# Moving the low-rank product, the evacuations and the late weight combinations of an adaptive FFN kernel

## The chip, the cores and the metric

One Trainium2 chip, one of its cores. The time is device microseconds of the whole program, the median of several runs. One execution of it was taken by the hardware profiler; times of single instructions come from that one, in microseconds from its start.

## The reference, cut to what matters

```python
# cond: a quantised weight with a low-rank part
lora_delta = lora_B @ lora_A * (32.0 / 64)               # rank 64, 2048 x 2048
cb    = codebook / max(abs(codebook))                    # 32 levels
scale = exp(scale_log)                                   # one per row and group of 128
normalized = (weight + lora_delta).reshape(O, I // 128, 128) / scale
thresholds = (cb[:-1] + cb[1:]) * 0.5
quantized  = cb[searchsorted(thresholds, normalized)]
w = (quantized - normalized) + normalized                # "straight through"
c = x @ ((w * scale).reshape(O, I) + lora_delta).T
# ffn: a dense layer, and 8 experts of rank 16 mixed by a router
result = c @ W_base.T + b_base
probs  = softmax(c @ router_w.T)
mixed  = einsum(einsum(c @ A_w.T, cores), probs)
out = x + result + (mixed @ B_w.T) * 2.0
```

x has 4096 rows of 2048, everything is float32.

## The kernel before, in words

The two dense layers and the residual are merged into one 2048 x 2048 matrix, M = W_base (w_q + delta) + identity, so that x meets only one large product. The program has three stretches.

**First stretch, the matrix (to about 1172 us).** It is built in 16 *strips* of 128 columns (loop at L755). Each strip quantises its 128 x 2048 piece of weight: for each of 27 thresholds ACT writes a mask (`raise_to`, L549: a Relu with a huge gain) and DVE writes the next level where the mask is set (L550, `copy_predicated`). The masks lie in a ring of four. The four lowest levels are not done by these passes, but ahead of time: ACT does level 0, and level 3 of half 0, in three parts each (`scalar_level`: Relu L516, Sign L519, then L521 or L524), GpSimd does levels 1 and 2, and sometimes 3, and adds them (`pool_levels` L534 and L535, `last_level` L539). From strip 6 on level 3 of half 1 is a half-width pass of DVE instead. While strip i goes through its passes, the other engines do:

- for strip i + 1: PE the low-rank product in two halves (`delta`, L410; both use the same PSUM tile), ACT its scaling (`scaled`, L502), GpSimd adding it and dividing by the scale (`normalize`, L504 to L507), and then the levels above;
- for strip i - 1: GpSimd turns the levels back into a weight (`straight_through`, L572 to L574, in two halves; in the last strip DVE in four quarters), PE multiplies it with W_base in two pairs of output blocks, (2, 0) and then (3, 1), in four quarters each (`products`, L621, `low_rank`, L609), PE the router's rows (`multiply_router`, L634 and L639; `router_sum`, L650), ACT copies the blocks out of PSUM and a DMA stores them (`keep`, L654 and L655);
- for strip i - 2: the last quarter of its (3, 1), and PE's router product with x (`route`, L674);
- from strip 5 on: GpSimd makes the sums of the finished columns that the fast product of the third stretch needs (`outer_w` L320, `inner_w` L329 to L332), and SP stores them (`put`, L351 to L353).

**Order of the work.** The program is in a manual schedule: each engine does its instructions in the order in which they are written. `behind(step, f, ...)` puts a piece of work after pass `step` of the strip; that fixes only its place in the queue of each engine that it uses. SP issues most DMAs in that order; GpSimd and ACT issue some of their own.

**Passage (1172 to about 1290 us).** After the last strip PE does its (2, 0), then its (3, 1). GpSimd fetches, sums and puts the sums of the first product's last quarter (`first_fetch` and so on). `late_columns` (L714) takes blocks 0 and 2 of the last group of strips: it fetches them into a buffer of 128 x 8192 ("late"), DVE makes the outer and inner sums of each block, and GpSimd issues the 32 DMAs that put them to DRAM. Then come the blocks 1 and 3 (`last_fetch`, L310 on SP for 1 and on GpSimd for 3, `last_outer`, `last_inner`, `last_put`), which the loop of the third stretch runs beside. The buffer of block 3 lies in memory that "late" used.

**Third stretch, the product (to the end).** x M is computed for four groups of 1024 tokens by a fast method of two levels, 7 x 7 = 49 products in each group (`product`, L954), with DVE, ACT and GpSimd adding up the results (`after`, L1034 to L1045) from four PSUM buffers. DVE's queue has, after the first terms of x, the sums of blocks 1 and 3 ("last"), then a difference of x (L917, xB), and then L1036 (u2), which frees the PSUM buffer that the seventh product needs.

The functions that the change touches, and where they are called:

Of the kernel before, what the change touches and what calls it, by code (L numbers as in the profile page):

```python
# [10 lines left out]
F32 = mybir.dt.float32  # L11
# [10 lines left out]
P = 128  # L22
# [6 lines left out]
NL = 4  # L29
# [154 lines left out]
def adaln_ffn_kernel(  # L184
# [29 lines left out]
    nc = tc.nc  # L214
    D, N = xT.shape
    NS, _, NM, _ = weight.shape
# [31 lines left out]
    NK = NS // 4  # L248
    HB = NK * 2

    strip = [j * NK + k for k in range(NK) for j in range(4)]
# [103 lines left out]
    def last_outer(b):  # L355
        outer_w(nc.vector, NK - 1, b)

    def last_inner(b, ms, z):
        inner_some(nc.vector, NK - 1, b, ms, z)

    def last_put(b, *sets):
        for ms in sets:
            put(NK - 1, b, ms, nc.gpsimd)


    with ExitStack() as sa:
# [22 lines left out]
        strips = {}  # L389
# [172 lines left out]
            assert not at, at  # L562

        def straight_through(i):
            last = i == NS - 1
            n = 4 if last else 2
            for h in range(n):
                m = ts(h, NM // n)
                w, a = strips[i]["w"][:, m, :], strips[i]["a"][:, m, :]
                sc = scale[:, strip[i], m].unsqueeze(2).to_broadcast([P, NM // n, P])  # L570
                v = nc.vector if last else nc.gpsimd
                v.tensor_tensor(a, a, w, ALU.subtract)  # L572
                v.tensor_tensor(a, a, w, ALU.add)  # L573
                v.tensor_tensor(a, a, sc, ALU.mult)  # L574
# [73 lines left out]
        def router_sum(i):  # L648

            nc.tensor.matmul(strips[i]["r"][:, P : P + RP], raw, stack, start=True, stop=True)  # L650

        def keep(i, b):
            out = spool.tile([P, 4, BC], F32, tag="out", name=f"out_{i}_{b}")
            nc.scalar.copy(out.rearrange("p q c -> p (q c)"), strips[i][b])  # L654
            (nc.scalar if i == NS - 1 else nc.sync).dma_start(wc_dram[i // 4][b][:, i % 4], out)  # L655

        def keep_router(i):
            nc.scalar.copy(rac[:, strip[i], :], strips[i]["r"][:, P : P + RP])
# [55 lines left out]
        def late_columns():  # L714

            t = big0.tile([P, NM, OQ], F32, tag="wb", name="late").rearrange("p m o -> p (m o)")
            for n, b in enumerate((0, 2)):
                f = t[:, 3584 * n : 3584 * n + 3584]
                columns(NK - 1, b, f[:, 0:2048], f[:, 2048:3584])
                fetch(NK - 1, b, range(3))  # L720
            for b in (0, 2):
                fetch(NK - 1, b, (3,))
            for b in (0, 2):
                if b == 0:
                    z = ypool.tile([P, 2048], F32, tag="up", name="late_z0")
                    z = (z[:, 0:1024], z[:, 1024:2048], t[:, 7168:8192])
                else:
                    more = ypool.tile([P, 1536], F32, tag="more", name="late_z1")
                    z = ypool.tile([P, 2048], F32, tag="up", name="late_z2")
                    z = (more[:, 0:1024], z[:, 0:1024], z[:, 1024:2048])  # L730
                last_outer(b)
                last_inner(b, (5, 6), z[0])
                last_inner(b, (2, 7), z[1])
                last_inner(b, (3,), z[2][:, 0:512])
                last_inner(b, (4,), z[2][:, 512:1024])
                last_put(b, (5, 6), (2, 7), (3,), (4,))


        made = {5: [(0, 0)], 6: [(0, 1)], 7: [(0, 2)], 8: [(0, 3)], 9: [(1, 0)], 10: [(1, 1)],
# [15 lines left out]
        for i in range(NS):  # L755
            at = {}

            def behind(r, f, *args):
                at.setdefault(r, []).append(lambda: f(*args))

            if i > 1:

                products(i - 2, (3, 1), NC - 1)
                route(i - 2, 0)
                behind(0, load_route, i - 2, 1)
                behind(2, keep, i - 2, 3)
                behind(3, keep, i - 2, 1)
            if i + 1 < NS:
                delta(i + 1, 0)
                if i > 0:  # L770
                    behind(1, load_w, i + 1, 2)
                behind(4, scaled, i + 1, 0)
                behind(4, normalize, i + 1, 0)
                behind(10, scaled, i + 1, 1)
                behind(10, normalize, i + 1, 1)
                for r, f, parts in ((0, 0, (11, 12, 13)), (NL - 1, 0, (14, 15, 18)), (0, 1, (19, 20, 21))):
                    for n, p in enumerate(parts):
                        behind(p, scalar_level, i + 1, f, r, n)
                behind(14, pool_levels, i + 1, 0)
                behind(19, last_level, i + 1, 0)  # L780
                behind(21, pool_levels, i + 1, 1)
            if i > 0:


                behind(9, load_route, i - 1, 0)
                if i == NS - 1:
                    behind(9, load_route, i - 1, 1)
                for c in range(2):
                    behind(2 + 3 * c, products, i - 1, (2, 0), c)
                if i + 1 < NS:  # L790
                    behind(7, delta, i + 1, 1)
                if i > 1:
                    behind(8, route, i - 2, 1)
                for c in range(2, NC):
                    behind(2 + 3 * c, products, i - 1, (2, 0), c)
                behind(13, multiply_router, i - 1)
                behind(16, keep, i - 1, 2)
                behind(17, keep, i - 1, 0)
                for c in range(NC - 1):
                    behind((17, 20, 22)[c], products, i - 1, (3, 1), c)  # L800
                behind(19, router_sum, i - 1)
                behind(23, keep_router, i - 1)
                behind(18, router_parts, i - 1)
                if i + 2 < NS:
                    behind(20, load_la, i + 2)
            else:
                behind(3, nc.vector.reciprocal, rflat[:, NM:], flat[:, NM:])
                behind(7, delta, i + 1, 1)
                behind(22, lora_columns, 0)
                behind(24, lora_columns, 1)  # L810
                behind(25, lora_router)
            for n, (g, b) in enumerate(made.get(i, [])):
                step_of = (3, 5, 10, 13, 17, 23, 25) if len(made[i]) == 1 else (
                    (4, 6, 8, 9, 10, 12, 13) if n == 0 else (17, 19, 21, 22, 23, 24, 25)
                )
# [12 lines left out]

                behind((0, 14)[n], begin, g, b)
                r = step_of  # L830
                behind(r[0], outer_w, nc.gpsimd, g, b)
                behind(r[1], inner_pair, g, b, PAIRS[0])
                behind(r[1], inner_pair, g, b, PAIRS[1])
                behind(r[2], put, g, b, PAIRS[0])
                behind(r[3], put, g, b, PAIRS[1])
                behind(r[4], inner_pair, g, b, PAIRS[2])
                behind(r[4], inner_pair, g, b, PAIRS[3])
                behind(r[5], put, g, b, PAIRS[2])
                behind(r[6], put, g, b, PAIRS[3])
            quantize(i, at)  # L840
            straight_through(i)

# [24 lines left out]
        for h in range(2):  # L867
            route(last, h)
# [412 lines left out]
```

## Time and profile before

| | |
|---|---|
| median of 3 runs | 2670.41 us (2669.06 to 2674.28) |
| the profiled execution | 2666.77 us, its span 2665.0 us |
| granted TensorE clock, mean | 0.975 of full speed |
| PE busy | 2503.9 us, 94% of the span |
| DVE busy | 1549.0 us, 58% |
| GpSimd busy | 1367.2 us, 51% |
| ACT busy | 1130.1 us, 42% |
| L550 on DVE, 448 passes | 1090.2 us busy |
| L549 on ACT, 448 masks | 872.4 us busy |
| DMA | 581 MB, 218 GB/s mean |

The page cuts the span into 40 slices of about 66.6 us. Each digit is the busy share in tenths:

```profile
PE   5499999999999999999999999999999999999999
DVE  9999999999999999973433223242133332224221
ACT  7899999999999999930000000000000000000000
POOL 5777778889888888745313140042320323202224
PEclk9799999999999999999999999999999999999999
```

PEclk is the clock that PE was granted, in tenths. The shares are averages over a slice: PE's 9 in the first stretch has some 5 us of idle time in each strip. In a row of the timeline, the numbers are start and duration, then engine, line, operation, shapes and how many instructions are taken together; in brackets stands the idle time of the engine before it and what ended it. In a row of the chain of waits there are start, duration and what was at work.

### The profile page before, as it was taken

How to read it: one execution, taken by the hardware profiler on the slowest of the kernel's cores; microseconds unless marked ns; L12 is line 12 of the kernel's file. 1: busy time of each engine (PE TensorE's matmuls, PEld its weight loads, DVE VectorE, ACT ScalarE, POOL GpSimd, SP SyncE). 2: the span in 40 equal slices, each digit the busy share in tenths (PEclk: the TensorE clock that was granted, in tenths of full speed). 3: DMA queues.
4: the chain of work that ended last, by engine and by line, in shares of the span. 5: the costliest groups of instructions: out<-in, count | busy, mean ns of one | idle time of the engine just before them, and what ended most of it. 6: DMA issues, size and time to landing. Idle time of an engine off the chain costs nothing.

```text
span 2665.0 us, 26423 instructions
## 1 busy us (share of the span) xinstructions
PE 2503.9 (94%) x10576; PEld 1704.1 (64%) x10576; DVE 1549.0 (58%) x990; ACT 1130.1 (42%) x796; POOL 1367.2 (51%) x783
## 2 busy tenths in 40 slices
PE   5499999999999999999999999999999999999999
PEld 2244444444444444345888888888888888888887
DVE  9999999999999999973433223242133332224221
ACT  7899999999999999930000000000000000000000
POOL 5777778889888888745313140042320323202224
PEclk9799999999999999999999999999999999999999
DMA  8255457776777777699844666536675455854554
GB/s 317 102 177 185 168 181 252 233 241 228 234 243 249 235 231 227 217 327 347 323 174 173 218 245 232 187 142 213 244 234 194 157 206 177 279 208 173 194 199 158
DMA packets 225979, 581.08 MB, mean 218 GB/s; under 512 B 20600, under 2 KB 121728, under 8 KB 182720
## 3 DMA queue, kind: packets, MB, share of 16 engines
q1 hardware_dynamic: 219296, 557.96, 61.1%
q0 software_dynamic: 4960, 14.95, 1.6%
q10 hardware_dynamic: 1600, 6.49, 0.7%
q8 instruction: 83, 1.36, 0.2%
q14 instruction: 40, 0.33, 0.0%
HBM read 477.62 MB, written 101.71 MB: 217 GB/s over the span
## 4 chain that ended last, share of the span: by engine, by line
PE 62%; ACT 17%; DVE 8%; POOL 7%; DMA 3%; issue 2%; SPq 0%; DVEq 0%; ACTq 0%; POOLq 0%
PE z L954 49%; ACT above L549 11%; PE m L621 10%; DVE a L550 7%; ACT sg L516 2%; ACT sg L519 2%; POOL a L572 1%; POOL a L573 1%; PE z L984 1%; ACT a L521 1%; POOL lv L534 1%; POOL a L574 1%; POOL a L535 1%; DMA xA<-in_xT 1%; DMA wc_dram<-out 1%
## 5 line engine op out<-in xcount | busy, mean ns | idle before, releaser
L550 DVE COPY_PREDICATED a<-above,step 128x2048 f32<-128x2048 uint8 (+1 forms) x448 | 1090.2, 2436 | 61.1 <-ACT above L549 19.3
L549 ACT ACTIVATE above<-w,neg_t 128x2048 fp8e5<-128x2048 f32 (+1 forms) x448 | 872.4, 1976 | 55.1 <-DVE a L550 44.5
L954 PE MATMUL z<-t,s 128*128 128x256 f32 x3584 | 791.4, 380 | 2.0 <-DVE u L1036 1.7
L954 PEld LDWEIGHTS z<-t,s 128*128 128x128 f32 x3584 | 677.5, 190 | 105.5 <-issue 13.2
L621 PE MATMUL m<-wbp,a 128*128 128x512 f32 x1024 | 502.1, 636 | 115.0 <-POOL a L574 101.0
L621 PE MATMUL m<-wb,a 128*128 128x512 f32 x1024 | 462.1, 594 | 4.4 <-ACT out L654 4.4
L621 PEld LDWEIGHTS m<-wbp,a 128*128 128x128 f32 x1024 | 202.6, 204 | 370.9 <-issue 239.7
L621 PEld LDWEIGHTS m<-wb,a 128*128 128x128 f32 x1024 | 194.5, 191 | 247.1 <-issue 242.4
L1034 ACT COPY m<-z 128x1024 f32<-128x1024 f32 x28 | 28.4, 1013 | 759.2 <-PE z L954 759.2
L1045 POOL TENSOR_TENSOR c<-u,m 128x1024 f32<-128x1024 f32 x16 | 50.1, 3130 | 443.8 <-DVE u L1042 422.4
L954 PE MATMUL z<-xA,s 128*128 128x256 f32 x1152 | 254.6, 379 | 0.0
L534 POOL TENSOR_SCALAR lv<-w,past,rise 128x1024 f32<-128x1024 f32 x65 | 245.9, 3783 | 3.7
L954 PEld LDWEIGHTS z<-xA,s 128*128 128x128 f32 x1152 | 218.8, 190 | 30.5 <-issue 0.8
L1045 POOL TENSOR_TENSOR M<-u,m 128x1024 f32<-128x1024 f32 x8 | 24.5, 3068 | 328.9 <-DVE u L1042 288.2
L954 PE MATMUL z<-xC,s 128*128 128x256 f32 x768 | 169.7, 379 | 0.0
L954 PE MATMUL z<-xB,s 128*128 128x256 f32 x768 | 169.7, 379 | 0.0
L535 POOL TENSOR_TENSOR a<-a,lv 128x1024 f32<-128x1024 f32 x65 | 154.3, 2374 | 27.1 <-ACT a L521 21.0
L1036 DVE TENSOR_TENSOR u<-z,m 128x1024 f32<-128x1024 f32 x28 | 34.3, 1224 | 218.5 <-issue 175.0
L1040 ACT COPY m<-z 128x1024 f32<-128x1024 f32 x28 | 28.3, 1011 | 308.8 <-PE z L954 308.8
L954 PEld LDWEIGHTS z<-xC,s 128*128 128x128 f32 x768 | 145.9, 190 | 19.8
L954 PEld LDWEIGHTS z<-xB,s 128*128 128x128 f32 x768 | 145.9, 190 | 19.8
L1042 DVE TENSOR_TENSOR u<-z,u 128x1024 f32<-128x1024 f32 x28 | 34.3, 1223 | 119.8 <-PE z L954 81.3
(213 smaller groups left out, 1958.0 us busy)
## 6 DMA issues: line engine op xcount, KB each, us to landing
s<-s_dram SPq DMA_DIRECT2D x196, 1024.0 KB, 4.9
wbp<-in_wbT SPq DMA_DIRECT2D x131, 1024.0 KB, 5.4
xs<-in_xT SPq DMA_DIRECT2D x64, 512.0 KB, 6.5
xA<-in_xT SPq DMA_DIRECT2D x24, 1024.0 KB, 9.4
s_dram<-z SPq DMA_DIRECT2D x84, 256.0 KB, 6.2
xB<-in_xT SPq DMA_DIRECT2D x16, 1024.0 KB, 10.4
outT<-M SPq DMA_DIRECT2D x16, 1024.0 KB, 12.5
w<-in_weight SPq DMA_DIRECT2D x30, 512.0 KB, 5.2
```

The lines of the kernel that those rows point to most:

```text
L516: nc.scalar.activation(strips[i]["sg"], q, AF.Relu, bias=neg_t[:, r : r + 1], scale=GAIN)
L519: nc.scalar.activation(sg, sg, AF.Sign)
L534: v.tensor_scalar(lv, half(i, f, "w"), past[:, r : r + 1], rise[:, r : r + 1], ALU.is_gt, ALU.mult)
L535: v.tensor_tensor(a, a, lv, ALU.add)
L549: nc.scalar.activation(above[:, c], q, AF.Relu, bias=neg_t[:, r : r + 1], scale=GAIN, saturate=False)
L550: nc.vector.copy_predicated(a, above[:, c].bitcast(U8), step[:, r : r + 1].to_broadcast([P, F // n]))
L621: nc.tensor.matmul(ps, strips[i]["a"][:, CM * c + m, :], t[:, m, :], start=c == 0 and m == 0, stop=False)
L954: nc.tensor.matmul(z[:, c, :], s[:, k, ts(c, P)], rhs[:, k, :], start=not more and k == 0 and c % PER == 0, stop=k == NK - 1 and c % PER = ...
L1034: nc.scalar.copy(temp("m1", o), z["a"])
L1036: nc.vector.tensor_tensor(temp("u2", o), z["b"], state["m1", o], ALU.add)
L1042: nc.vector.tensor_tensor(temp("u3", o), z["d"], state["u2", o], ALU.add)
L1045: lambda d: nc.gpsimd.tensor_tensor(d, state["u3", o], state["m5", o], ALU.add),
```

## The change

It moves work and splits some; the passes, the products and the sums stay the same.

- `straight_through` on GpSimd works in a quarter, a quarter and a half of the strip's width, instead of two halves.
- The second half of the low-rank product (`delta(i + 1, 1)`) comes behind the first quarter of (2, 0) instead of the second; the quarters of (2, 0) are put behind steps 4, 6, 8, 11 (before 2, 5, 8, 11), `scaled` at 3 and 7 (4 and 10), `normalize` at 5 and 9 (4 and 10).
- The passes of the lowest levels come in another order and at other steps; `pool_levels` at 13 and 19 (14 and 21), `last_level` at 23 (19).
- `keep` of blocks 2 and 0 at 14 and 15 (16 and 17), of block 1 at 4 (3); `router_sum` at 20 and `keep_router` at 24 (19 and 23).
- The combinations' steps: outer sums at 4 (3), inner pairs at 8, 10, 24, 25 (5, 5, 17, 17), puts at 10, 12, 25, 26 (10, 13, 23, 25).
- In the passage both blocks are copied out of PSUM first, then the router's part, then both stores are issued on ACT's queue; the router's sum comes after the first quarter of (3, 1).
- `late_columns`: both blocks' outer sums first; block 0's inner sums on DVE, block 2's sixteen inner operations on GpSimd, in two batches; the eight puts of the second batch come last.

```diff
-    def last_inner(b, ms, z):
-        inner_some(nc.vector, NK - 1, b, ms, z)
+    def last_inner(b, ms, z, v=nc.vector):
+        inner_some(v, NK - 1, b, ms, z)
...
         def straight_through(i):
             last = i == NS - 1
-            n = 4 if last else 2
-            for h in range(n):
-                m = ts(h, NM // n)
+            v = nc.vector if last else nc.gpsimd
+            for m in (0, 4), (4, 8), *(((8, 12), (12, 16)) if last else ((8, 16),)):
...
-        def keep(i, b):
+        def evacuate(i, b):
             out = spool.tile([P, 4, BC], F32, tag="out", name=f"out_{i}_{b}")
             nc.scalar.copy(out.rearrange("p q c -> p (q c)"), strips[i][b])
-            (nc.scalar if i == NS - 1 else nc.sync).dma_start(wc_dram[i // 4][b][:, i % 4], out)
+            strips[i]["out", b] = out
+
+        def store(i, b, q=nc.sync):
+            q.dma_start(wc_dram[i // 4][b][:, i % 4], strips[i]["out", b])
+
+        def keep(i, b):
+            evacuate(i, b)
+            store(i, b)
...
                 last_outer(b)
-                last_inner(b, (5, 6), z[0])
-                last_inner(b, (2, 7), z[1])
-                last_inner(b, (3,), z[2][:, 0:512])
-                last_inner(b, (4,), z[2][:, 512:1024])
-                last_put(b, (5, 6), (2, 7), (3,), (4,))
+            z = ypool.tile([P, 2048], F32, tag="up", name="late_z0")
+            last_inner(0, (5, 6), z[:, 0:1024])
+            last_inner(0, (2, 7), z[:, 1024:2048])
+            last_inner(0, (3,), t[:, 7168:7680])
+            last_inner(0, (4,), t[:, 7680:8192])
+
+            z = ypool.tile([P, 1536], F32, tag="more", name="late_z1")
+            last_inner(2, (5, 6), z[:, 0:1024], nc.gpsimd)
+            last_inner(2, (3,), z[:, 1024:1536], nc.gpsimd)
+            for b in (0, 2):
+                last_put(b, (5, 6))
+            last_put(2, (3,))
+            last_put(0, (2, 7), (3,), (4,))
+            z = ypool.tile([P, 2048], F32, tag="up", name="late_z2")
+            last_inner(2, (2, 7), z[:, 0:1024], nc.gpsimd)
+            last_inner(2, (4,), z[:, 1024:1536], nc.gpsimd)
+            last_put(2, (2, 7), (4,))
...
-                behind(3, keep, i - 2, 1)
+                behind(4, keep, i - 2, 1)
...
-                behind(4, scaled, i + 1, 0)
-                behind(4, normalize, i + 1, 0)
-                behind(10, scaled, i + 1, 1)
-                behind(10, normalize, i + 1, 1)
-                for r, f, parts in ((0, 0, (11, 12, 13)), (NL - 1, 0, (14, 15, 18)), (0, 1, (19, 20, 21))):
+                behind(3, scaled, i + 1, 0)
+                behind(5, delta, i + 1, 1)
+                behind(7, scaled, i + 1, 1)
+                behind(5, normalize, i + 1, 0)
+                behind(9, normalize, i + 1, 1)
+                for r, f, parts in ((0, 0, (11, 12, 13)), (0, 1, (16, 17, 19)), (NL - 1, 0, (20, 21, 23))):
...
-                behind(14, pool_levels, i + 1, 0)
-                behind(19, last_level, i + 1, 0)
-                behind(21, pool_levels, i + 1, 1)
+                behind(13, pool_levels, i + 1, 0)
+                behind(19, pool_levels, i + 1, 1)
+                behind(23, last_level, i + 1, 0)
...
-                    behind(2 + 3 * c, products, i - 1, (2, 0), c)
-                if i + 1 < NS:
-                    behind(7, delta, i + 1, 1)
+                    behind((4, 6, 8, 11)[c], products, i - 1, (2, 0), c)
...
-                behind(16, keep, i - 1, 2)
-                behind(17, keep, i - 1, 0)
+                behind(14, keep, i - 1, 2)
+                behind(15, keep, i - 1, 0)
...
         for bs in ((2, 0), (3, 1)):
             for c in range(NC):
                 products(last, bs, c)
+                if bs[0] == 3 and c == 0:
+                    router_sum(last)
+                    keep_router(last)
+            for b in bs:
+                evacuate(last, b)
             if bs[0] == 2:
                 multiply_router(last)
                 router_parts(last)
             for b in bs:
-                keep(last, b)
+                store(last, b, nc.scalar)
             if bs[0] == 2:
-                router_sum(last)
-                keep_router(last)
                 late_columns()
```

More of the change, by code (lines that the diff above doesn't have):

```diff
@@ L565, in straight_through @@
             last = i == NS - 1
-            n = 4 if last else 2
-            for h in range(n):
-                m = ts(h, NM // n)
+            v = nc.vector if last else nc.gpsimd
+            for m in (0, 4), (4, 8), *(((8, 12), (12, 16)) if last else ((8, 16),)):
+                n = m[1] - m[0]
+                m = slice(*m)
                 w, a = strips[i]["w"][:, m, :], strips[i]["a"][:, m, :]
-                sc = scale[:, strip[i], m].unsqueeze(2).to_broadcast([P, NM // n, P])
-                v = nc.vector if last else nc.gpsimd
+                sc = scale[:, strip[i], m].unsqueeze(2).to_broadcast([P, n, P])
                 v.tensor_tensor(a, a, w, ALU.subtract)
@@ L723, in late_columns @@
             for b in (0, 2):
[L724 to L730, printed above, removed]
-                last_outer(b)
-                last_inner(b, (5, 6), z[0])
-                last_inner(b, (2, 7), z[1])
-                last_inner(b, (3,), z[2][:, 0:512])
-                last_inner(b, (4,), z[2][:, 512:1024])
-                last_put(b, (5, 6), (2, 7), (3,), (4,))
+                last_outer(b)
+            z = ypool.tile([P, 2048], F32, tag="up", name="late_z0")
[14 more added lines that the diff above has]
+            last_put(2, (2, 7), (4,))
         made = {5: [(0, 0)], 6: [(0, 1)], 7: [(0, 2)], 8: [(0, 3)], 9: [(1, 0)], 10: [(1, 1)],
@@ L794, in adaln_ffn_kernel @@
                 for c in range(2, NC):
-                    behind(2 + 3 * c, products, i - 1, (2, 0), c)
+                    behind((4, 6, 8, 11)[c], products, i - 1, (2, 0), c)
                 behind(13, multiply_router, i - 1)
-                behind(16, keep, i - 1, 2)
-                behind(17, keep, i - 1, 0)
+                behind(14, keep, i - 1, 2)
+                behind(15, keep, i - 1, 0)
                 for c in range(NC - 1):
                     behind((17, 20, 22)[c], products, i - 1, (3, 1), c)
-                behind(19, router_sum, i - 1)
-                behind(23, keep_router, i - 1)
+                behind(20, router_sum, i - 1)
+                behind(24, keep_router, i - 1)
                 behind(18, router_parts, i - 1)
@@ L807, in adaln_ffn_kernel @@
                 behind(3, nc.vector.reciprocal, rflat[:, NM:], flat[:, NM:])
-                behind(7, delta, i + 1, 1)
                 behind(22, lora_columns, 0)
@@ L812, in adaln_ffn_kernel @@
             for n, (g, b) in enumerate(made.get(i, [])):
-                step_of = (3, 5, 10, 13, 17, 23, 25) if len(made[i]) == 1 else (
-                    (4, 6, 8, 9, 10, 12, 13) if n == 0 else (17, 19, 21, 22, 23, 24, 25)
+                step_of = ((4, 8, 10), (4, 10, 12), (4, 24, 25), (4, 25, 26)) if len(made[i]) == 1 else (
+                    ((4, 6, 8), (6, 6, 9), (10, 10, 12), (10, 10, 13)) if n == 0 else
+                    ((17, 19, 21), (19, 19, 22), (23, 23, 24), (23, 23, 25))
                 )
@@ L830, in adaln_ffn_kernel @@
                 r = step_of
[L831 to L839, printed above, removed]
+                behind(r[0][0], outer_w, nc.gpsimd, g, b)
+                for k, pair in enumerate(PAIRS):
+                    behind(r[k][1] if k else r[0][1], inner_pair, g, b, pair)
+                    behind(r[k][2], put, g, b, pair)
             quantize(i, at)
```

## The prediction

> **What bounds the kernel now.** I read the page's slices first: DVE is at 9 tenths up to about 1170 us, PE from there on. So there are two stages, and a third short one between them, where both rows dip. Then I read the waits, by engine.
>
> ```profile
> DVE a L550 <- ACT above L549: 19.3, 49, 0.6
> ACT a L502 <- PE d L410: 49.8, 14, 5.5
> ACT out L654 <- PE m L609: 38.1, 4, 26.5
> ```
>
> Columns: total, times, longest, in us. In the first stage DVE runs 448 predicated copies almost without a break: 2.575 us from one start to the next. A strip with 27 passes has to take 69.5 us, one with a half pass more 70.85; the starts of the strips from 6 on lie 70.7 to 72.0 apart. All that the schedule can win there is the 19.3 us in which DVE waits for ACT's mask, less 0.1 us of handover for each of the 49 waits: 14.4 us. ACT in turn loses 49.8 us to the low-rank product on PE (L410). Strip 11 shows how the two hang together. First PE, then ACT, then DVE:
>
> ```profile
> 822.09 6.16 PE L621 MATMUL m<-wbp,a 128*128 128x512 f32 x8 [4.75 <-POOL a L574]
> 838.71 1.16 PE L410 MATMUL d<-la,lora_BT_sb 64*128 64x128 f32 x16
> 839.92 1.02 ACT L502 ACTIVATE a<-d 128x1024 f32<-128x1024 f32 x1 [3.12 <-PE d L410]
> 874.09 7.63 DVE L550 COPY_PREDICATED a<-above,step 128x2048 f32<-128x2048 uint8 x3 [0.55 <-ACT above L549]
> ```
>
> ACT's mask takes 1.90 us of pitch where DVE takes 2.575, so ACT gains 0.675 us of lead per pass, up to about 5.6 us (four masks). The stall of 3.12 us and some 13 us of other ACT work per strip use it up, and late in the strip DVE waits three times for 0.2 to 0.6 us.
>
> The second thing is the passage between the stages, by the chain of waits:
>
> ```profile
> 1226.21 0.70 DVE late L320
> ...
> 1253.65 6.98 DMA s_dram<-late
> ...
> 1263.80 10.44 DMA last<-wc_dram
> 1274.31 0.70 DVE last L320
> ...
> 1287.34 1.15 DVE u L1036
> 1288.53 11.49 PE z L954 x52
> ```
>
> The last put of the late combinations lands at 1260.63, only then does GpSimd's queue let go the last fetch (it takes over that memory), which lands at L = 1274.23. DVE then has 10.7 us of combinations, 2.35 us of xB and 1.2 us of u2 ahead of PE's seventh product, which starts at L + 14.3. From there PE has no idle time of note, so the end moves with that point.
>
> **The change, part by part.** Times are of the profiled execution: span 2665.0, 2666.77 in all, 3.6 below the median 2670.41.
>
> *Strips: straight_through in 512-, 512- and 1024-wide pieces.* A half costs GpSimd 2.38 + 2.37 + 1.90 = 6.65 us before PE may start; the first quarter 1.28 + 1.28 + about 1.0 = 3.56. PE starts 3.1 us earlier: 819.0 in strip 11. The three added GpSimd operations cost about 0.4 us of starts. GpSimd is at 7 to 9 tenths here; normalize follows a step later, and nothing of it is needed before ACT's first level pass at step 11. If that cover failed, these 0.4 us would come once per strip, 6 us in all; the trace has GpSimd waiting there for ACT (L506 for L502, 34.9 us), which now ends sooner.
>
> *delta(i+1,1) after one quarter instead of two.* From 819.0: first quarter 9.7 (a cold start, 6.16 + 0.2 + 3.45), delta 1.1, so done at 829.8 instead of 839.9. `scaled` half 1 goes from step 10 to 7, so ACT is there about 3 × 2.575 earlier, at 829.1. Of 3.12 us of stall, about 0.7 to 1 stay.
>
> *keep(i-1,2) at step 14 instead of 16.* It needs the whole of (2,0): 33.7 us after PE's start by the trace (822.09 to 855.78), so 852.7. ACT, by its ledger (1.90 per mask, scaled 0.90, Relu 1.04, Sign 0.95, level 1.14), comes to it at about 847.7. What was a wait of zero becomes one of 4.6 to 5 us, and behind it in ACT's queue are all the masks. Carried on to step 26 with a lead of 0.3 us at the restart, the ledger gives 0.78 us of DVE gaps in a strip, where 0.86 are there now. One stall is exchanged for another. That is ten strips at about +0.1 to +0.2 us.
>
> *Levels' passes, combinations and puts at other steps.* As many ACT, GpSimd and SP instructions as before, in another order. On ACT the last level of half 0 goes behind the first of half 1, on GpSimd the levels of half 1 come from step 21 to 19 and last_level from 19 to 23; on SP the stores of keep go ahead of two puts, and the last two puts to 25 and 26. DVE waits for none of these within the strip, only GpSimd's levels of half 1 are due at its end, and these come earlier. I take nothing; bounds -2 and +3 (a head gap of 0.2 in each strip if GpSimd is late with last_level).
>
> *Strips 1 to 5.* Here no combinations disturb, and GpSimd's levels start one step earlier (13): the head gaps of 0.3 to 0.65 us go. Strip 1 has 11 gaps now (4.57 us with handovers) and keeps about half: +1.8. Strip 2 loses 0.7 (it has none now and gets the new stall). Strips 3 to 5 win 2 to 4. Sum of the first stage: 1.8 - 0.7 + 2…4 + 1…2: G = **4 us**, bounds 0 and 14.4.
>
> Here a rule is to be weighed. PE's first group after 4.48 to 5.60 us idle takes 5.56 to 6.34 us in these strips, after 3.45 us idle 3.70:
>
> ```profile
> 180.23 3.70 PE L621 MATMUL m<-wbp,a 128*128 128x512 f32 x8 [3.45 <-POOL a L574]
> ```
>
> The Trainium skill, "TensorE: Matmul & The Clock Gate", section "What's actually happening", has the array back at half clock after at least one idle window of about 3.4 us, the window running freely; so an idle of 3.45 us may go either way, and 4.75 nearly always goes cold. PE's work in a strip does not change and the period hardly does, so about 5 us idle stay and I take cold. If the idle is spread over two places and the head stays below 3.4, (2,0) is done 2.5 us earlier, at 850.2; the stall at step 14 is then 2.5 and the ledger shows no gaps: G = 14. This is the first rival's door.
>
> *Passage: both evacuations first, stores after them on ACT's queue.* Now:
>
> ```profile
> 1215.74 5.40 PE L621 MATMUL m<-wb,a 128*128 128x512 f32 x8 [4.43 <-ACT out L654]
> ```
>
> ACT's second copy stands behind ACT's own store, issued at 1214.72, which waited for a DMA slot that the second half of xA held until 1214.64. With both copies first that wait (4.43) and the slow restart (1.8) go, and PE gets to its second stage up to 6 us earlier. It gains nothing at the end: the seventh product waits for L, and the 1.71 us stall that is there grows by what PE wins. The stores themselves still wait for 1214.7; the second is issued some 0.6 us earlier. The router's evacuation moved behind the first quarter is PE and ACT time beside all this: nothing.
>
> *Late combinations.* Now DVE starts at S = 1226.21, and L = S + 48.0. In the new order: both outer sets on DVE 5.24; GpSimd's (5,6) and (3) of block 2, 4 × 0.735 + 4 × 0.46 = 4.8; and 0.8 for meeting DVE's block-0 work (below); then 24 puts at 0.71 = 17.1; about 1 for a DMA slot and the memory of late_z0; (2,7) and (4), again 4.8; the eighth of the last puts 5.2 later; landing 6.5 to 7; four fetch issues 2.4; landing 9.5 to 10.4. Sum about 57.8. So **+9.8**: the second batch of GpSimd's arithmetic and the eight puts behind it stand in the queue where DVE did the same (5.6 us in all) ahead of a queue that was never empty. S itself moves: -0.65 (stores back to back) and -2 (in the last strip PE's third quarter, and with it GpSimd's and SP's chain to the xA load, comes 0 to 3 earlier). L relative to the end of the strips: +9.8 - 0.65 - 2 = **+7**, bounds +5 and +10.
>
> A second rule, against this part: the skill's "SBUF — State Buffer", section "Who interferes with whom", says that a DVE operation with two SBUF inputs and a GpSimd operation that reads SBUF exclude each other, the second waiting for the whole of the first. The rows:
>
> ```profile
> 1172.59 1.24 POOL L332 TENSOR_TENSOR z<-more,z 128x256 f32<-128x256 f32 x1
> 1178.16 0.79 POOL L330 TENSOR_TENSOR z<-z,more 128x128 f32<-128x128 f32 x1
> 1173.28 1.10 DVE L573 TENSOR_TENSOR a<-a,w 128x512 f32<-128x512 f32 x1
> ```
>
> Alone these take 0.735, 0.46 and 0.69. Each loses 0.3 to 0.5 us where they meet, less than the whole of the other. By the row GpSimd's first batch (eight operations beside DVE's sixteen) costs 0.5 to 1.6 us more; by the rule up to 5.6, DVE's whole work on block 0. I take 0.8; the rule's end is the upper bound.
>
> **Sum.** 2666.8 - 4 + 7 = 2669.8, that is +3; at the median, 2670.4 + 3: **2673**. A measurement here tells 0.2% (5.3 us) from no change, so this is "no difference", nearer to slower than to faster.
>
> **Rivals.**
> *Faster: the strips close up.* For it: the stall of 3.12 us that starts each strip's loss is removed, and the pot of 14.4 us is real. Against it: step 14 for keep. If PE starts warm, or ACT comes later to step 14 than I reckon, G = 10 to 14; with L + 6 the end is -4 to -8: about 2664.
> *Slower: GpSimd's queue decides L.* The place is GpSimd's queue between S and the last fetch, the price ten us and more. It decides from L - S = 60, if the strips give 4, and from 56 if they give nothing (the break-even with G = 4 is 54.7). With puts at 0.78, contention at the rule's end and slots late (S + 62) and G = 0: +11, 2681.
> *The passage does what its code says.* If L does not bind (the last fetch is let go earlier than I think, because its memory belongs to another put), PE's 4.43 + 1.8 + 1.71 = 7.9 us come through whole, and with G = 4 the end is 2659. Against it: the trace has the fetch at 1261.37, 0.74 us after the last put's landing.
>
> **How the numbers follow.** The forecast (L + 7, strips 4): 0.45, of it 0.37 within 0.2% and 0.08 slower. Strips close up: 0.20, of it 0.17 faster and 0.03 within. GpSimd's queue, strips nothing: 0.28, slower. The passage comes through: 0.07, of it 0.05 faster. Together faster 0.22, within 0.2% 0.42, slower 0.36. Range 2664 to 2682: it takes the strips' rival at its middle and the queue's rival to its end; 0.1 stays out at each side. The likeliest case's own range is 2668 to 2678.
>
> **What would show it.** In a strip: the wait of L502 for PE's d falls from 3.12 to about 1, and a new one of 4 to 5 us stands before keep's copy at step 14; DVE's gaps stay, at the last five passes; PE's first group still takes about 6 us. If that group takes 3.7 and DVE's gaps are gone, the first rival holds. In the passage: PE's wait of 4.43 is gone, and PE's wait before the seventh product of the second stage is 12 to 16 us, for DVE's u2. L - S is 56 to 60; under 52 my sum of GpSimd's queue is wrong, and the end is earlier. The prediction is wrong altogether if PE shows no such wait, or new idle time later in the second stage.

## The result, and the profile after

The changed kernel takes 2681.12 us in the median of 6 runs (2679.56 to 2684.15), beside 2670.16 for the kernel before (2669.06 to 2674.28): **0.4% slower**, ratio 1.004, 95% interval 1.0028 to 1.0051. The prediction was 2673 in a range of 2664 to 2682. The time lies inside, but near its upper end, and what came true is the rival "slower", to which I had given 0.28, not the likeliest case. So the number fell inside thanks to a range whose upper end was drawn for that rival, not thanks to the forecast.

The profiled execution took 2680.74 us, its span 2678.9, 13.9 more than the span before. (The profiled execution before was 3.4 us under the median of its kernel, so this difference is 3 us larger than that of the medians.) The waits after, as total, times, longest in us:

```profile
ACT out L655 <- PE m L610: 130.9, 18, 36.1
PE z L964 <- DVE u L1046: 17.2, 1, 17.2
DVE a L550 <- ACT above L549: 22.9, 50, 2.1
ACT a L502 <- PE d L410: 13.8, 14, 2.7
POOL last L310 <- DMA s_dram<-late: 9.3, 1, 9.3
```

ACT's wait for the low-rank product fell from 49.8 to 13.8, as it should. But its waits before its copies of finished blocks rose from 38.1 to 130.9. Of the 130.9, 71.3 are new ones for (2, 0) at step 14, 4.3 to 5.7 us in each of the strips 1 to 15 (before, one of 2.9 in strip 15); nearly all of the rest lies in the passage. And DVE's wait for masks did not fall (19.3 before). Strip 11 shows the exchange; PE's rows, then ACT's:

```profile
822.37 5.67 PE L622 MATMUL m<-wbp,a 128*128 128x512 f32 x8 [5.85 <-POOL a L575]
831.62 1.16 PE L410 MATMUL d<-la,lora_BT_sb 64*128 64x128 f32 x16
832.83 1.02 ACT L502 ACTIVATE a<-d 128x1024 f32<-128x1024 f32 x1 [0.44 <-PE d L410]
855.86 0.59 ACT L655 COPY out<-m 128x512 f32<-128x512 f32 x1 [4.26 <-PE m L610]
```

The strip starts at 818.40 here and at 815.04 before, so PE starts 3.97 us into it instead of 7.05, and the wait at L502 is 0.44 instead of 3.12. At L655 ACT now stands 4.26 us. In strip 2, which had no gap at all before, it stands longer, and DVE runs dry (ACT's row, then DVE's):

```profile
210.06 0.59 ACT L655 COPY out<-m 128x512 f32<-128x512 f32 x1 [5.64 <-PE m L610]
212.57 5.03 DVE L550 COPY_PREDICATED a<-above,step 128x2048 f32<-128x2048 uint8 x2 [2.14 <-ACT above L549]
```

The last pass ends at 1176.0 instead of 1172.5. The passage, by the chain of waits:

```profile
1228.69 0.70 DVE late L320
...
1269.67 9.23 DMA s_dram<-late
...
1281.99 4.44 DMA last<-wc_dram
1286.51 0.70 DVE last L320
...
1299.52 1.15 DVE u L1046
1300.71 9.33 PE z L964 x34
```

S to L is 57.7 us, 48.0 before. PE's wait of 4.43 in the passage is gone, its first product of the last stretch starts at 1240.86, 3.7 us earlier in spite of the later strips; and then it waits for the seventh, and starts that one cold (the granted clock is 0.50 from 1300.7 to 1304.2, and full after that):

```profile
1300.71 8.89 PE L964 MATMUL z<-t,s 128*128 128x256 f32 x32 [17.18 <-DVE u L1046]
```

So 13.9 = 3.5 (strips) + 9.7 (S to L) - 1.0 (end of the strips to S) + 1.7 (the group takes 8.89 instead of 7.17).

### The profile page after: what moved, and what is told of

It reads as the page before. It is cut to its first block, busy times and chain, and to the rows that moved or that the text cites. A ratio compares the mean times of both kernels' runs of the same rounds, so it can differ in the third digit from the quotient of the medians.

```text
span 2678.9 us, 26464 instructions
## 1 busy us (share of the span) xinstructions
PE 2503.6 (93%) x10576; PEld 1703.9 (64%) x10576; DVE 1551.9 (58%) x974; ACT 1125.6 (42%) x796; POOL 1385.5 (52%) x844
## 4 chain that ended last, share of the span: by engine, by line
PE 70%; ACT 12%; DVE 10%; DMA 4%; POOL 3%; issue 1%; SPq 0%; DVEq 0%; ACTq 0%; POOLq 0%
PE z L964 49%; PE m L622 17%; DVE a L550 9%; ACT above L549 8%; PE z L994 1%; ACT sg L516 1%; ACT sg L519 1%; DMA xA<-in_xT 1%; DMA wc_dram<-out 1%; POOL a L573 1%; POOL a L574 1%; PE d L410 1%; ACT a L521 1%; POOL a L575 1%; PE m L610 1%
## 5 line engine op out<-in xcount | busy, mean ns | idle before, releaser
L550 DVE COPY_PREDICATED a<-above,step 128x2048 f32<-128x2048 uint8 (+1 forms) x448 | 1090.7, 2438 | 64.1 <-ACT above L549 22.9
L964 PE MATMUL z<-t,s 128*128 128x256 f32 x3584 | 793.2, 381 | 17.9 <-DVE u L1046 17.2
L1055 POOL TENSOR_TENSOR c<-u,m 128x1024 f32<-128x1024 f32 x16 | 49.8, 3112 | 443.5 <-DVE u L1052 422.3
```

The costliest lines, as they stand in the source:

```text
L550: nc.vector.copy_predicated(a, above[:, c].bitcast(U8), step[:, r : r + 1].to_broadcast([P, F // n]))
L964: nc.tensor.matmul(z[:, c, :], s[:, k, ts(c, P)], rhs[:, k, :], start=not more and k == 0 and c % PER == 0, stop=k == NK - 1 and c % PER = ...
L1055: lambda d: nc.gpsimd.tensor_tensor(d, state["u3", o], state["m5", o], ALU.add),
```

## The experiments

Three numbers tell these kernels apart (of one profiled execution each): the end of the last pass on DVE; from there to DVE's first operation on the last fetched block ("to L"); and PE's wait before the seventh product. S by itself is not steady: in executions with the same passage it lay 48.8 to 54.4 us behind the last pass, and L - S made up for only a part of that. With the late combinations all on DVE "to L" is 98.5 to 104.5, with block 2's on GpSimd 110.5 to 113.0. All are measured against the kernel before, run beside them (its medians were 2670.2 to 2671.3).

| kernel | median us | ratio, 95% interval | last pass ends | to L | PE's wait |
|---|---|---|---|---|---|
| before | 2670.2 | | 1172.5 | 101.8 | 1.7 |
| changed | 2681.1 | 1.004 (1.0028–1.0051) | 1176.0 | 110.5 | 17.2 |
| e1_keep16 | 2665.8 | 0.9982 (0.9976–0.9989) | 1159.5 | 110.7 | 16.5 |
| e2_late_dve | 2672.4 | 1.0005 (0.9998–1.0011) | 1176.8 | 99.7 | 6.1 |
| e3_evac | 2671.0 | 1.0001 (0.9993–1.0009) | 1172.3 | 100.3 | 4.5 |
| e4_both | 2655.9 | 0.995 (0.9937–0.9962) | 1159.7 | 99.5 | 4.2 |
| e5_late_pool | 2683.4 | 1.0044 (1.0032–1.0057) | 1175.1 | 113.0 | 12.8 |
| e6_block2_first | 2659.1 | 0.9951 (0.9939–0.9964) | 1158.8 | 101.2 | none |
| e7_order_dve | 2678.9 | 1.0032 (1.002–1.0045) | 1174.4 | 104.5 | none |
| e8_keep15 | 2666.4 | 0.9984 (0.9976–0.9991) | 1160.4 | 110.5 | 16.7 |
| e9_halves | 2657.6 | 0.995 (0.9937–0.9962) | 1162.6 | 103.7 | 8.8 |
| e11_two_tiles | 2653.5 | 0.9933 (0.9921–0.9945) | 1160.2 | 98.5 | none |
| e4_again | 2656.2 | 0.9943 (0.9929–0.9956) | 1159.6 | 103.0 | 3.6 |

### keep later again: e1_keep16

```diff
-                behind(14, keep, i - 1, 2)
-                behind(15, keep, i - 1, 0)
+                behind(16, keep, i - 1, 2)
+                behind(17, keep, i - 1, 0)
```

> The changed kernel with keep of blocks 2 and 0 of strip i-1 back at steps 16 and 17. Theory (the evacuation of block 2 at step 14 comes before PE has finished (2, 0), and stops all the masks behind it in ACT's queue): ACT's wait there, 4.26 us in strip 11 and 5.64 in strip 2, goes to about 0, DVE's waits for masks fall from 22.9 us to under 8, the end of the last pass from 1176.0 to 1162-1166, and the whole run to 2667-2671. Rival (the new order of the levels' passes takes ACT's lead): the waits of DVE stay above 17 us and the time stays at 2678-2682.

The last pass ends at 1159.5, 16.5 us earlier than in the changed kernel, and the run takes 2665.8. Of the waits of DVE for masks one of 0.5 us is left:

```profile
DVE a L550 <- ACT above L549: 0.5, 1, 0.5
```

In strip 11 ACT reaches L655 after PE, with no wait. Both gains are a little larger than expected. The rest of the strips' rearrangement is a good one; the two steps by which these two evacuations were moved cost it 15 us.

### One step later: e8_keep15

The same edit with 15 and 16.

> The changed kernel with keep of block 2 at step 15 and of block 0 at 16, one step later. Theory (what counts is how long ACT stands before PE has finished (2, 0), against its lead of about 5.6 us): the wait in strip 11 goes from 4.26 to 1.7-2.2 us, which the lead covers, so that DVE's waits for masks fall from 22.9 to under 5 us and the run to 2665-2669, as with keep at 16 and 17. Rival (any wait there costs its length): DVE's waits 10-14 us, run 2672-2676.

```profile
843.27 0.59 ACT L655 COPY out<-m 128x512 f32<-128x512 f32 x1 [3.10 <-PE m L610]
```

```profile
DVE a L550 <- ACT above L549: 2.6, 7, 0.4
```

The wait was longer than I reckoned (3.10 in strip 11, 1.9 to 3.8 over the strips), yet DVE feels almost nothing of it: 2.6 us in the whole run, 2666.4. The price of an ACT wait here is not its length. Strips 2 to 4 show it best: with a wait of at most 0.8 us (e1_keep16) a strip took 69.5 us on average, with one of 3.8 (this run) 70.1, with one of 5.6 (the changed kernel) 72.1. So the first 3 us cost 0.6, the next 1.9 cost 2.0: ACT's lead covers most of a wait up to some length, and nearly nothing beyond it.

### The late combinations back on DVE: e2_late_dve

The changed kernel with the old `late_columns`.

> The changed kernel with the late combinations as before: all on DVE, block by block, puts in the old order. Theory (GpSimd's queue between DVE's start S and the landing L of the last fetch is on the path): L - S falls from 57.7 to about 48 us, PE's wait before the seventh product from 17.2 to about 7, and the run to 2669-2672. Rival (the passage's loss lies ahead of S, in the stores and the reloads of blocks 0 and 2): L - S as it is, 2679-2682.

L - S is 47.7, to L it takes 99.7 instead of 110.5 us, and the run 2672.4, 8.7 less. PE's wait has gone down from 17.2, but not away:

```profile
1290.71 9.18 PE L959 MATMUL z<-t,s 128*128 128x256 f32 x32 [6.07 <-DVE u L1041]
```

### The evacuations alone: e3_evac

The kernel before with `evacuate` and `store` as in the change, and the router's sum behind the first quarter of (3, 1), only for the last strip.

> The kernel before with nothing but the two evacuations ahead of the router and the stores in the passage, and the router's sum behind the first quarter of (3, 1). Theory (L sets the start of the seventh product): PE's wait of 4.43 us goes, its wait before the seventh product grows from 1.7 to 7-9 us and the group after it restarts cold, +1.7; S is 0.6 earlier; run 2669-2673, no difference. Rival (PE's earlier end comes through): 2662-2664.

2671.0, ratio 1.0001. PE's 4.43 us and its restart are saved, and PE gives them back in front of the seventh product:

```profile
1286.82 8.86 PE L964 MATMUL z<-t,s 128*128 128x256 f32 x32 [4.48 <-DVE u L1046]
```

It had 1.7 us of wait there and a group of 7.17. The wait grew less than expected (4.5, not 7 to 9) because L came 1.7 us earlier in this execution and because PE stood 2.4 us before its second product, but the end is where it was.

### The late combinations alone: e5_late_pool

The kernel before with the new `late_columns`.

> The kernel before with nothing but the new late combinations (block 2's inner sums on GpSimd, the new order of the puts). Theory (they cost what L - S grows by, and the cold restart behind the longer wait): L - S 57 to 58 instead of 48, PE's wait before the seventh product 11 to 12, run 2680-2684. Rival (the loss in the passage needs the early evacuations too): 2670-2674.

2683.4. L - S is 59.7, above the expected 57 to 58. PE waits for the same thing as in the changed kernel, and the whole loss is there without any other part of the change:

```profile
1302.31 9.77 PE L959 MATMUL z<-t,s 128*128 128x256 f32 x32 [12.78 <-DVE u L1041]
```

Its strips, which are those of before, end at 1175.1, 2.6 us later, with 23.0 us of waits for masks. So the sum of these waits differs between executions of the same strips: 17.3, 19.3 and 23.0 in the three traces with the old ones, 22.2 to 23.5 in the three with the new ones and keep at 14. The strips' loss of 3.5 us between the two main profiles is thus partly that spread; by the means of three each it is 2.4. Strip 2 shows where the spread comes from. It takes 71.3 us here, 69.6 in the other two, and its first group, after the same idle time, takes 5.40 instead of the 3.70 that they had. So the low-rank product behind it is late, ACT waits 3.84 us for it at L502 instead of the 2.16 of before, and DVE gets gaps where it had none:

```profile
179.85 5.40 PE L621 MATMUL m<-wbp,a 128*128 128x512 f32 x8 [3.46 <-POOL a L574]
```

### Engine or order: e7_order_dve

```diff
-            last_inner(2, (5, 6), z[:, 0:1024], nc.gpsimd)
-            last_inner(2, (3,), z[:, 1024:1536], nc.gpsimd)
+            last_inner(2, (5, 6), z[:, 0:1024])
+            last_inner(2, (3,), z[:, 1024:1536])
...
-            last_inner(2, (2, 7), z[:, 0:1024], nc.gpsimd)
-            last_inner(2, (4,), z[:, 1024:1536], nc.gpsimd)
+            last_inner(2, (2, 7), z[:, 0:1024])
+            last_inner(2, (4,), z[:, 1024:1536])
```

> The changed kernel with block 2's sixteen inner operations on DVE again, but in the new order, with the new order of the puts and the new buffers. It tells the engine from the order. If GpSimd's arithmetic in front of its own puts is all of the cost, L - S falls from 57.7 to about 48 and the run to 2670-2673. If the order has a part (no put can go before both outer sums and block 0's inner sums are done, and the second batch waits for the buffer that the first puts hold), L - S is 52 to 55 and the run 2675-2679. If only the order counts, 2680-2682.

The time, 2678.9, is as the middle case had it, but not for its reason: L - S is only 50.4. Of the 9.7 us by which L - S had grown, GpSimd's arithmetic thus makes 7.3 and the order about 2.4 (from one execution of each). The cost of the order sits elsewhere. In the new order the second batch needs the buffer that the first puts read, and on DVE it holds up the x terms queued behind it, so that PE stops before its second product (not before the seventh, so the table has no wait there). DVE's row, then PE's:

```profile
1256.96 0.42 DVE L329 TENSOR_TENSOR late_z<-late 128x256 f32<-128x256 f32 x1 [16.15 <-DMA s_dram<-late]
```

```profile
1262.00 15.65 PE L964 MATMUL z<-t,s 128*128 128x256 f32 x64 [14.49 <-issue]
```

The new order of the puts is bad with either engine: on DVE its wait for the buffer stops PE, on GpSimd it goes into L.

### Both undone: e4_both, e4_again

keep at 16 and 17, and the old `late_columns`.

> The changed kernel with both undone: keep at 16 and 17, and the late combinations as before. Theory: the two gains add up, -11 and -10 to the changed kernel: 2656-2661, some 10-14 us under the kernel before. Rival (the gain of the strips is eaten in the passage, since the loads there do not move with it): 2664-2670.

> The version with keep at 16 and 17 and the old late combinations once more, beside the other two on the same chip: 2654-2658.

2655.9 and 2656.2: the two gains add up (25.2 us under the changed kernel, 15.3 and 8.7 alone), and this is 0.5% faster than the kernel before. What is left of the change in the strips (the quarter pieces, the low-rank product behind the first quarter, the new steps of the levels and the sums) is worth the 13 us by which its last pass ends earlier than before.

### The pieces of straight_through: e9_halves

```diff
-            for m in (0, 4), (4, 8), *(((8, 12), (12, 16)) if last else ((8, 16),)):
+            for m in ((0, 4), (4, 8), (8, 12), (12, 16)) if last else ((0, 8), (8, 16)):
```

> The version with keep at 16 and 17 and the old late combinations (2655.9), with straight_through in two halves again. Theory (PE's start sets when the low-rank product and (2, 0) are done): PE starts 3.1 us later in a strip, ACT's wait for PE's d at L502 in strip 11 is 3 to 4 us instead of under 1, the lead covers most of that since it comes at step 7, and DVE's waits for masks rise from 0.5 to 3-12 us: run 2658-2666. Rival (the place of the low-rank product alone matters, the quarter pieces do nothing): 2655-2657.

```profile
825.57 1.02 ACT L502 ACTIVATE a<-d 128x1024 f32<-128x1024 f32 x1 [4.87 <-PE d L410]
```

The low-rank wait is there (4.87, more than the 3 to 4 expected), DVE's waits are 5.3 us, the last pass ends 2.9 us later than in e4_both. The run, 2657.6, is 0.4 under the expected range and within the spread of e4_both and e4_again: by the trace the pieces are worth 3 us, by the run times it can't be told. The last pass still ends 9.9 us earlier than before. No run tells which of the other moves does that, the place of the low-rank product or the new steps. Shorter waits for that product are not the reason: ACT's waits at L502 sum to 59.7 us in this run, more than the 49.8 before, and DVE hardly feels them at their new step.

### The order of the blocks: e6_block2_first

The loops over the last fetches, the sums and the puts of the two blocks run as (2, 0).

> The version with keep at 16 and 17 and the old late combinations on DVE (2655.9), with block 2 of the late combinations and its puts ahead of block 0. Theory (the last fetch waits for the landing of the puts that read block 2's part of the late buffer): GpSimd no longer waits before L310 (5.7 us now), L - S goes from 49.5 to 40-43, PE's wait of 4.2 before the seventh product and the cold restart after it go: 2648-2652. Rival (the fetch waits for block 0's puts just as well, since its memory reaches into both): no difference, 2654-2657.

The rival held as to the wait: GpSimd still stands 5.2 us for a put before L310. But the run takes 2659.1, 2 us more than the rival had, since block 0's sums now wait for a put to land and PE stands 9.1 us before its second product. DVE's row, then PE's:

```profile
1232.73 0.42 DVE L329 TENSOR_TENSOR late_z<-late 128x256 f32<-128x256 f32 x1 [11.54 <-DMA s_dram<-late]
```

```profile
1240.17 15.99 PE L959 MATMUL z<-t,s 128*128 128x256 f32 x64 [9.13 <-issue]
```

One reading is left: the late buffer is one tile, and the fetch waits for the last put that reads it, whichever block that is. The next run tests it.

### Two tiles: e11_two_tiles

```diff
-            t = big0.tile([P, NM, OQ], F32, tag="wb", name="late").rearrange("p m o -> p (m o)")
+            t = [
+                big0.tile([P, NM // 2, OQ], F32, tag="wb", name=f"late_{b}").rearrange("p m o -> p (m o)")
+                for b in (0, 2)
+            ]
             for n, b in enumerate((0, 2)):
-                f = t[:, 3584 * n : 3584 * n + 3584]
+                f = t[n]
...
-                    z = (z[:, 0:1024], z[:, 1024:2048], t[:, 7168:8192])
+                    z = (z[:, 0:1024], z[:, 1024:2048], t[0][:, 3584:4096], more[:, 1024:1536])
```

> The same version, with the late buffer (and the part of W_base that lies there before) as two tiles of half the width, one for each block, so that the last fetch takes over only block 0's. Block 2's last inner set goes to its own tile, one of block 0's to the other small buffer. Theory (the fetch waits for the landing of the last put only since the memory is one tile): GpSimd's 5.7 us before L310 go, L - S falls from 49.5 to 41-44, PE's wait of 4.2 before the seventh product and the cold restart go: 2648-2652. Rival (then something else on DVE or SP is late for the seventh product): 2653-2657.

```profile
1245.49 2.12 POOL L310 DMA_DIRECT2D last<-wc_dram  x3 [0.50 <-DMA s_dram<-late_z]
```

```profile
1258.84 7.14 PE L969 MATMUL z<-t,s 128*128 128x256 f32 x32 [1.63 <-DMA s<-s_dram]
1265.82 7.07 PE L969 MATMUL z<-xA,s 128*128 128x256 f32 x32
1272.83 7.17 PE L969 MATMUL z<-t,s 128*128 128x256 f32 x32
```

The wait for the landing fell from 5.7 to 0.5 us, and the seventh product (the third row) follows the sixth with no gap. The run takes 2653.5 (2651.1 to 2654.0, e4_both and e4_again together 2654.1 to 2658.7): 2.6 us better, less than the 4 to 8 expected and where the rival had it. L - S is 45.8 instead of 41 to 44, and PE now waits 2.3 us before its second product and 1.63 for a load of s before the fourth. It is the fastest version found, 0.67% under the kernel before.

## Why the prediction was right or wrong

**Right: the earlier start and the exchange in a strip from 6 on.** I had PE's start 3.1 earlier (measured: 3.08), the wait at L502 at 0.7 to 1 (0.44), the new wait before keep's copy at 4.6 to 5 (4.26), and gaps on DVE as large as before (strip 11 takes 71.7 us in both). e1_keep16 showed that the wait at step 14 was the cause.

**Wrong: the first stage's G = 4.** It failed in "*Strips 1 to 5*", where I took +1.8 - 0.7 + 2…4. From one strip's first pass to the next one's, strip 1 did gain 1.6. Strip 2 lost 2.7 (I had 0.7), and strips 3 to 5 lost 1.6 together, where I had them win 2 to 4; strips 6 to 15 lost 0.7, where I had 1 to 2 won. I had carried ACT's ledger through step 14 for strip 11 alone, and credited the early strips with the removed wait; the new one I charged to strip 2 only, and too small. It is longer there (5.6 us in strips 2 to 4), and DVE feels it in the same strip: in strip 2 by a gap of 2.14 and four more of 0.3 to 0.4. G was -3.5 between the two profiles, -2.4 by the means: 6.4 to 7.5 us of the error. About 1.7 us of strip 2's loss hangs on the clock: the profile of before had its quick group of 3.70 there; against e5_late_pool, with the same strips but without that luck, strip 2 lost 1.0 and the whole stage 0.9.

**Wrong in the first rival, too.** I had "PE starts warm" as its first door. Nothing of it came: in e4_both, where the idle time ahead of PE's first group was 2.79 to 5.79 us, that group took 5.28 to 6.63 us in each of the strips 2 to 15. The strips close up with a cold PE, by a keep that comes later.

**Right: L decides the passage.** The early evacuations alone changed nothing (e3_evac), the late combinations alone cost all of it (e5_late_pool), and taken out of the change they gave 8.7 back (e2_late_dve). PE's wait before the seventh product was 17.2, above my 12 to 16, since L came 8.7 us later behind the strips (I had 7) and PE's own work was 7.2 earlier behind them (I had up to 6). What I had not seen is that L binds by only 2.4 us. DVE stood 33.75 us (12.93 before) in front of its last x term until a put had landed. That was at 1278.9, when the put landed that held the last fetch:

```profile
1278.88 1.23 DVE L942 TENSOR_TENSOR t<-t,xA 128x1024 f32<-128x1024 f32 x1 [33.75 <-DMA s_dram<-late_z]
```

From there it was busy to 1284.1, and then waited 2.41 us for L. A faster fetch alone could have won no more than that; the puts hold up both.

**Right by cancelling: L - S of 57.8 (57.7).** Its terms were not. These rows of the changed kernel give them; GpSimd's queue first, DVE's last:

```profile
1232.73 1.09 POOL L329 TENSOR_TENSOR late_z<-late 128x256 f32<-128x256 f32 x1 [11.42 <-DVE late L320]
...
1258.60 0.77 POOL L352 DMA_DIRECT2D s_dram<-late  x1 [1.05 <-DMA s_dram<-late_z]
1259.36 0.55 POOL L353 DMA_DIRECT2D s_dram<-late  x1
1259.93 0.74 POOL L329 TENSOR_TENSOR late_z<-late 128x256 f32<-128x256 f32 x1
...
1269.67 0.55 POOL L353 DMA_DIRECT2D s_dram<-late  x1
1279.55 2.15 POOL L310 DMA_DIRECT2D last<-wc_dram  x3 [9.32 <-DMA s_dram<-late]
```

```profile
1234.30 0.94 DVE L329 TENSOR_TENSOR late_z<-late 128x256 f32<-128x256 f32 x1
```

GpSimd's first batch began before the outer sums were through (S + 4.0, not 5.2), and took 6.3 (4.8 + 0.8 expected). The 24 puts took 20.9 instead of 18.1, since they waited four times for an earlier put to land. From the last put to the fetch there were 9.9 us instead of 6.5 to 7. The last part of the fetch then landed in 4.4 instead of 9.5 to 10.4; SP had no load to issue beside it, where before it was issuing three loads of s. The errors add up to about -0.1. That is luck, and the next sum may not have it.

**Left out: the cold restart behind the longer wait**, +1.7. I had named a slow restart of 1.8 in the passage, and did not carry it to the place to which the wait moved. **Mis-sized: S**, -2.65 expected against -1.0, which the spread of S between executions does not let me tell apart.

**The rule on shared reads.** Both engines lost time where they met, as the rows foretold. GpSimd's operation of 0.735 took 1.09 beside the outer sums, DVE's of 0.42 took 0.94; over the batch GpSimd lost 1.5 us against its 4.8 alone, DVE 2.4 against the 4.8 that its sixteen took in e7_order_dve. My 0.5 to 1.6 for GpSimd held; waiting for all of DVE's work, 5.6, did not come. I had not charged DVE's part.

## What to carry to other kernels

When a step is moved forward, ask for every engine that it uses whether its input is ready there, and carry the answer through each kind of stage, not only through the one that was looked at; a wait in a queue that feeds the bottleneck costs little up to the lead, and nearly its whole length beyond it (waits of 1.9 to 3.8 us at step 15 left DVE 2.6 us of waiting in the whole run, those of 4.3 to 5.7 at step 14 left 22.9). A stall that goes away is a gain only if what the engine meets next is earlier as well: PE's 4.43 us came back in front of the seventh product. A sum that meets the measured total may still be made of wrong terms, so compare the terms.

## What the runs showed of the hardware that I had not expected

The 24 puts from GpSimd's queue were issued about 0.73 us apart at first; of the last ten, four waited 0.5 to 1.2 us for an earlier one to land. So a put in a long row costs more than its issue. And the row that I took for a threshold was none. Before, PE's idle time of 3.45 us was followed by a group of 3.70, in e5_late_pool 3.46 by one of 5.40. In e4_both a shorter idle time and a longer one were both followed by cold groups:

```profile
243.73 5.40 PE L622 MATMUL m<-wbp,a 128*128 128x512 f32 x8 [2.79 <-POOL a L575]
313.14 5.28 PE L622 MATMUL m<-wbp,a 128*128 128x512 f32 x8 [3.84 <-POOL a L575]
```

The granted clock tells more. Each row below is a stretch of about 3.4 us: its length, the busy time of PE, weight loads, DVE, ACT and GpSimd (with counts), then the granted clock, the share of the DMA engines and GB/s. The first two are of e4_both, the others of before:

```profile
241.20:244.70 3.50, 0.97 (x2) 0.49 (x3) 3.40 (x2) 3.50 (x4) 3.34 (x4) 1.00 0.80 287
244.70:248.10 3.40, 3.40 (x5) 1.33 (x4) 3.19 (x3) 3.19 (x4) 3.24 (x4) 0.50 0.00 0
```

```profile
175.10:178.50 3.40, 1.68 (x24) 0.97 (x16) 3.30 (x2) 3.40 (x4) 3.24 (x3) 1.00 0.52 133
178.50:182.00 3.50, 1.77 (x4) 0.87 (x5) 3.29 (x3) 3.50 (x3) 3.50 (x2) 1.00 0.46 178
```

In e4_both the clock went to half only about 1 us after PE had started again, for one such stretch, and the idle time had lain in one stretch, in which PE was busy for 0.97 us. In before the idle time was split over two stretches, PE was busy for half of each, and the clock stayed full. So the length of the idle time alone did not decide, which fits the freely running window of which the Trainium skill speaks ("TensorE: Matmul & The Clock Gate", section "What's actually happening"); but the window need not be idle as a whole, as 2.79 us, less than its 3.4, were enough. How much work keeps the clock up these traces do not settle: in another stretch of the trace of before (141.0 to 144.4) PE was busy for 1.68 us too, and the clock was 0.50 after it. In the strips 2 to 15 of all 13 traces only three such first groups were warm, all in strip 2: those of before and e3_evac, after 3.45 us idle, and that of e11_two_tiles, after 2.55.
